# Places given out block by block and token numbers scattered to lists, with three feed-forward groups for the last image

## The chip, the cores and the metric

The kernel runs on one core of a Trainium2 chip. The metric is the device time of one execution in microseconds (us); a kernel's time is the median of its runs. TensorE is written PE, VectorE DVE, ScalarE ACT, GpSimd POOL and SyncE SP, as in the profile.

## The reference

One metaformer layer on x of shape 4 x 256 x 64 x 64, all in float32:

```python
x = x + conv_ref(_ln_c(x))          # three modulated deformable 3x3 convolutions, each with relu
t = _to_tokens(x)                   # 4 images x 4096 tokens x 256 channels
t = t + ffn_ref(_ln_t(t))           # mixture of experts
x = _from_tokens(t, x)
```

Each deformable layer computes offsets and a mask by an ordinary 3x3 convolution (27 outputs), samples its input bilinearly at 9 moved positions per pixel, and multiplies the 9 x 256 samples by its weights. The feed-forward part has 8 experts of 256 -> 512 -> 256 with exact GELU. A softmax over the logits of a gate picks the two best experts of a token and weighs their outputs. The reference computes all experts for all tokens; the kernel computes only the two that count.

## The kernel before

**The convolutions.** An image has 8 blocks of 512 pixels (4 tiles of 128). The list `stages` in `run` (line 1102) sets the order of (layer, image, first block, last block), 96 blocks in all; I write (2,1) 3 for layer 2, image 1, block 3. A block has 9 taps, and `main_block` (line 503) does for each tap 4 gathers, `samples` (515): an indirect DMA on POOL's queue (line 524) brings for each of 128 pixels one table row of 4 KB, two operations on DVE (530, 535) and one on ACT (538) blend it to a sample. There are 9 buffers for gathered tiles (`GB`) and 8 for samples. `turn` (542) transposes pairs of samples on PE (553) and ACT copies them out (556); `share` (562) multiplies them by the weights (570). `finish` (580) applies the ReLU on ACT, two instructions a block (601). `off_block` (358) computes offsets, indices and coefficients for a later block, `store_table` (326) and `enter` (344) write the rows of the next layer's table, `pre_block` (450) loads an image, normalises its pixels over the channels (`normalise`, 58), writes the first table and transposes back (483).

**What is done beside them.** Such work is written as generators. `aside` (1064) puts each one's steps into one of two lists, `side` and `plans_side`; after each tap `step` (1068) takes from each list as many steps as will empty it by the end of the block. So a list of 12 steps gives two in some taps, and a list of `tokens` and `pre_block` steps shares its taps. `after(self.last)` places an instruction behind the newest sampling operation of its engine, `after(self.gathered)` behind the newest gather on POOL.

**Tokens.** After a block of layer 2, `tokens` (611) adds x, transposes to 512 tokens, normalises them, writes them to DRAM (`z`), and computes logits, probabilities, ranks of the experts (`rk`) and the two weights (`cw`).

**The feed-forward part.** The tokens are handled in groups: images 0 to 2 are a group each, image 3 is two groups of 4 blocks. When a group's last block has its ranks, `enqueue` (1026) puts into the lane `routes`: `route` (714), which gives each token its two slots in lists ordered by expert; then for each tile `invert` (827), which turns the slots into the lists of token numbers: two comparisons on DVE (836, 838) make one-hot matrices in float16, and PE multiplies them (842), accumulating in PSUM; then `begin` (1034). A list is cut into units of 128 rows. A group of M tiles has 2M + 7 units, done in steps of two units (a pair) or one (a single): 40 steps and 71 units for an image, 24 steps and 39 units for half of one. `expert` (887) does a step: `fetch` (851) brings on POOL's queue the expert's weights (line 861, unless the same are there already) and one tile of tokens per unit (874); PE transposes them (904) and multiplies (918, 936) with GELU on ACT (928) between. `products` (945) adds the bias on DVE (955) and writes the rows to DRAM. When the group's steps are done, `end` (1043) fills the lane `sums`: for each tile two indirect DMAs on POOL (981) gather its two results (`gy`), DVE adds them with their weights (996), PE transposes (1014), and the rows are written out.

**The pace.** The lanes get one credit per tap (`pump`, 1059). A group's `pace` is the number of taps that a pair takes: 5, 6, 2, 1.5 and 0 for the five groups. At the end of a layer whose next stage needs it (after (1,3) and after (2,3)) `settle` (1079) empties the side lists, and after the last block `drain` (1088) runs what is left. Instructions of an engine run in the order in which the program has them, POOL's DMAs included.

Of the kernel before, what the change touches and what calls it, by code (L numbers as in the profile page):

```python
# [41 lines left out]
NW = 3  # L42
LEAST = 2.0**-30
# [14 lines left out]
def normalise(nc, pool, src, dst, eps, nm):  # L58
# [16 lines left out]
    for _ in range(3):  # L75
        nc.vector.tensor_tensor(sq, rs, rs, ALU.mult)
        nc.vector.scalar_tensor_tensor(sq, sq, -0.5, ve, ALU.mult, ALU.mult)
        nc.vector.scalar_tensor_tensor(rs, sq, 1.5, rs, ALU.add, ALU.mult)
    yield rs
    for t in range(T):  # L80
        nc.vector.tensor_scalar(
            dst[:, t, :], src[:, t, :], mv[:, t, 0:1], rs[:, t : t + 1], ALU.subtract, ALU.mult
        )


class Group:


    def __init__(self, b, n0, n1):
# [8 lines left out]
        self.zt, self.acc, self.gy, self.sums, self.py = {}, [], [], [], None  # L98
        self.order = [self.starts[s % NW] + s // NW for s in range(self.NF)]
# [7 lines left out]
class Lane:  # L107
# [5 lines left out]
    def put(self, taps, fn):  # L113
        self.pieces.append((taps, fn))
# [11 lines left out]
class Weave:  # L126
# [3 lines left out]
    def __init__(self, ctx, tc, ins, out):  # L130
# [29 lines left out]
        self.side, self.plans_side = [], []  # L160
# [58 lines left out]
    def ffn_constants(self):  # L219
# [9 lines left out]
        for g in self.groups:  # L229
            g.zd = self.dram.tile([g.M * P, C], F32, name=f"z_{g.nm}", tag=f"z_{g.nm}")  # L230
        self.ys = [
# [28 lines left out]
        self.fresh = {}  # L260
        for M in {g.M for g in self.groups}:
            fresh = cst.tile([P, E, M], F32, name=f"fresh_{M}")
            nc.vector.memset(fresh, 1.0)
            nc.vector.memset(fresh[:, :, 0:1], 0.0)
            self.fresh[M] = fresh
# [10 lines left out]
        self.token = {}  # L276
        for M in {g.M for g in self.groups}:
            assert M * P // 2 <= 2048
            token = cst.tile([P, M], F32, name=f"token_{M}")
            nc.vector.tensor_scalar(  # L280
                token, self.row_f[:, :M], float(P), self.part, ALU.mult, ALU.add
            )
            nc.vector.tensor_scalar(token, token, float(M * P // 2), None, ALU.subtract)
            self.token[M] = token


# [163 lines left out]
    def pre_block(self, b, n, wins, spare, spill=0):  # L450
# [19 lines left out]
        rest = normalise(nc, self.small, h, h, EPS_C, nm)  # L470
# [140 lines left out]
    def tokens(self, b, n, r):  # L611
# [4 lines left out]
        if n == grp.n0:  # L616
            grp.cw = self.rt2.tile([P, 2, grp.M], F32, tag="cw", bufs=3, name=f"cw_{grp.nm}")
            grp.rk = self.rt2.tile([P, E, grp.M], F32, tag="rk", name=f"rk_{grp.nm}")
        xc = self.big.tile([P, CC, BLK], F32, tag="a", name=f"xr_{nm}")
# [32 lines left out]
        rest = normalise(nc, self.small, tok, z, EPS_T, nm)  # L652
# [54 lines left out]
        for i in range(2):  # L707
            w = small("lg", (P, TPB, E))
            nc.vector.scalar_tensor_tensor(w, rk, float(i), pr, ALU.is_equal, ALU.mult)
            nc.vector.tensor_reduce(grp.cw[:, i, m0 : m0 + TPB], w, AX.X, ALU.add)  # L710
        if n == grp.n1 - 1:
            self.enqueue(grp)

    def route(self, grp):

        nc, M, NF = self.nc, grp.M, grp.NF
        grp.slots = self.rt2.tile([P, 2, M], I32, tag="slots", bufs=3, name=f"slots_{grp.nm}")
        grp.tok = self.rt2.tile([P, grp.NU], I32, tag="tok", name=f"tok_{grp.nm}")
        grp.wrow = self.rt2.tile([P, NF], I32, tag="wrow", name=f"wrow_{grp.nm}")

        def small(tag, shape, dt=F32):
            return self.rt.tile(list(shape), dt, tag=tag, name=f"{tag}_{grp.nm}")

        both = small("r0", (P, E, M))
        nc.vector.tensor_scalar(both, grp.rk, 1.0, None, ALU.is_le)
        rp = self.ps.tile([P, 2, E, M], F32, tag="tp", name=f"rp_{grp.nm}")
        nc.tensor.matmul(rp[:, 0], lhsT=self.upper, rhs=both, start=True, stop=True)
        nc.tensor.matmul(rp[:, 1], lhsT=self.ones, rhs=both, start=True, stop=True)
        tot = small("r1", (P, E, M))
        nc.vector.tensor_copy(tot, rp[:, 1])  # L730
        slot = small("r2", (P, E, M))
        nc.vector.tensor_tensor_scan(
            slot.rearrange("p e m -> p (e m)"),
            self.fresh[M].rearrange("p e m -> p (e m)"),
            tot.rearrange("p e m -> p (e m)"),
            0.0, ALU.mult, ALU.add,
        )

        ni = small("ni", (P, E), I32)
        nc.vector.tensor_scalar(ni, slot[:, :, M - 1], float(P - 1), None, ALU.add)  # L740
# [8 lines left out]
        for v in range(2):  # L749
# [11 lines left out]
        cut = small("cut", (P, E))  # L761
        nc.vector.tensor_scalar(cut, nt[:, 0], float(FT), None, ALU.mult)
        nc.vector.tensor_tensor(off[:, 1], off[:, 1], cut, ALU.subtract)
        nc.vector.tensor_tensor(off[:, 1], off[:, 1], off[:, 0], ALU.subtract)
        nc.vector.tensor_scalar(end[:, 0], end[:, 0], float(FU), None, ALU.mult)
        nc.vector.tensor_scalar(end[:, 1], end[:, 1], base, None, ALU.add)
        nc.vector.tensor_tensor(slot, slot, tot, ALU.subtract)
        nc.vector.tensor_tensor(slot, slot, rp[:, 0], ALU.add)
        every = [P, E, M]
        over = small("r1", (P, E, M))  # L770
        nc.vector.tensor_tensor(over, slot, cut.unsqueeze(2).to_broadcast(every), ALU.is_ge)
        nc.vector.tensor_tensor(
            over, over, off[:, 1].unsqueeze(2).to_broadcast(every), ALU.mult
# [3 lines left out]
            slot, slot, off[:, 0].unsqueeze(2).to_broadcast(every), ALU.add  # L777
# [9 lines left out]

# [6 lines left out]
        part = small("exv", (P, NF))  # L794
        for v in range(2):
            past = small("r1", (P, NF, E))
            nc.vector.tensor_tensor(
                past,
                first.unsqueeze(2).to_broadcast([P, NF, E]),
                end[:, v].unsqueeze(1).to_broadcast([P, NF, E]),  # L800
                ALU.is_ge,
            )
            nc.vector.tensor_reduce(part if v else ex, past, AX.X, ALU.add)
        nc.vector.scalar_tensor_tensor(ex, ex, float(E), ex, ALU.is_lt, ALU.mult)
        nc.vector.tensor_tensor(ex, ex, part, ALU.add)
# [9 lines left out]
        nc.vector.tensor_copy(grp.wrow, rows)  # L815


        grp.digits = []
        for v, (op, k) in enumerate(((ALU.bitwise_and, P - 1), (ALU.logical_shift_right, 7))):
            di = small("di", (P, 2, M), I32)  # L820
            nc.vector.tensor_scalar(di, grp.slots, k, None, op)
            df = small(f"df{v}", (P, 2, M))
            nc.vector.tensor_copy(df, di)
            grp.digits.append(df)
        grp.inv = self.ps1.tile([P, grp.NU], F32, tag="py", name=f"inv_{grp.nm}")

    def invert(self, grp, m):


        nc = self.nc  # L830
        lo, hi = grp.digits
        n = grp.NU
        for i in range(2):
            nm = f"{grp.nm}_{m}_{i}"
            at = self.ffn.tile([P, P], F16, tag="at", name=f"at_{nm}")
            nc.vector.tensor_scalar(at, self.row_f, lo[:, i, m : m + 1], None, ALU.is_equal)
            num = self.ffn.tile([P, n], F16, tag="num", name=f"num_{nm}")
            nc.vector.tensor_scalar(
                num, self.row_f[:, :n], hi[:, i, m : m + 1], self.token[grp.M][:, m : m + 1],
                ALU.is_equal, ALU.mult,  # L840
            )
            nc.tensor.matmul(
# [369 lines left out]
```

## Time and profile before

| What | Value |
|---|---|
| median of 3 runs | 6431.33 us (6419.34 to 6440.2) |
| the profiled execution | 6426.59 us |
| its span, first to last instruction | 6424.5 us |
| mean granted clock of PE | 0.973 |
| software queue (POOL's DMAs): packets, MB, share of 16 engines | 550,240, 1971.12, 81.2% |
| hardware queue (SP's DMAs): the same | 249,136, 270.82, 12.3% |
| HBM traffic over the span | 367 GB/s |

A row of the costliest groups reads: line, engine, operation, written tile <- read tiles, count | busy us in total, mean ns of one | idle time of the engine just before them, and what ended most of it. The page's row of 40 slices gives the busy share in tenths through the run:

```profile
PE   7999999889899999999889999999987999987987
...
POOL 4666776666777767667777776767777764667644
...
DMA  8999999999899999999899999999999996899854
```

Means of single instructions on the lines named above: fetch of weights (861) 1059 ns x168 of POOL's time, of a tile of tokens (874) 1006 ns x291, of results (981) 1081 ns x256; one of the small operations of `tokens` on DVE (709, 128x32) 201 ns.

In time, the last ReLU ends at 6080 us of the span, the last of the products (line 955) starts at 6372 us, and POOL issues the last group's 32 gathers of results from about 6375 to 6415 us.

### The profile page before, as it was taken

The page shows a single profiled execution, that of the slowest core. Times are in us where ns is not written, and L with a number is a line of the kernel's source. Part 1 is how long each engine was busy: PE and PEld are TensorE (multiplying, and loading weights), DVE is VectorE, ACT ScalarE, POOL GpSimd, SP SyncE. Part 2 cuts the span into 40 slices and gives each one's busy share as a digit, 9 for nine tenths or more (in the row PEclk, how much of TensorE's full clock was granted, in tenths as well). Part 3 has the DMA queues.
Part 4 walks back from the last instruction along what each step waited for, and adds up shares of the span by engine and source line. Part 5 has one row for each costly group of instructions (what it writes and reads, how often), then busy time and mean ns, then how long its engine had stood idle before and what let it go on. Part 6 is the DMA issues. An engine that isn't in the chain of part 4 may idle for free.

```text
span 6424.5 us, 88218 instructions
## 1 busy us (share of the span) xinstructions
PE 5903.1 (92%) x26358; PEld 3413.5 (53%) x26358; DVE 4954.5 (77%) x11575; ACT 3298.7 (51%) x7154; POOL 4396.0 (68%) x4215
## 2 busy tenths in 40 slices
PE   7999999889899999999889999999987999987987
PEld 3444444444455555665445555555643566644675
DVE  7988888888977768888877877778988764678621
ACT  3555555555555555555455555555654544454422
POOL 4666776666777767667777776767777764667644
PEclk8999999899999999999999999999999999999998
DMA  8999999999899999999899999999999996899854
GB/s 286 388 370 378 408 404 401 377 361 365 325 393 372 366 340 399 391 355 364 315 356 366 393 380 352 385 368 380 387 369 345 346 338 235 322 335 341 314 179 145
DMA packets 799851, 2247.56 MB, mean 350 GB/s; under 512 B 102184, under 2 KB 300456, under 8 KB 790544
## 3 DMA queue, kind: packets, MB, share of 16 engines
q0 software_dynamic: 550240, 1971.12, 81.2%
q1 hardware_dynamic: 249136, 270.82, 12.3%
q8 instruction: 212, 3.47, 0.2%
q14 instruction: 263, 2.15, 0.1%
HBM read 2166.72 MB, written 191.81 MB: 367 GB/s over the span
## 4 chain that ended last, share of the span: by engine, by line
PE 67%; DVE 11%; DMA 10%; issue 5%; ACT 4%; POOL 2%; SPq 0%; DVEq 0%; ACTq 0%; POOLq 0%
PE acc L570 33%; PE tp L553 9%; DMA g<-tab,idx 8%; PE ph L918 7%; PE py L936 7%; PE po L378 6%; DVE g L530 4%; DVE s L535 3%; ACT s L538 2%; PE pm L392 1%; POOL g L524 1%; PE lp_tok L642 1%; ACT win L601 1%; PE ftp L904 1%; PE tpv L338 1%
## 5 line engine op out<-in xcount | busy, mean ns | idle before, releaser
L524 POOL DMA_INDIRECT g<-tab,idx x3456 | 3625.0, 1049 | 1553.5 <-issue 595.8
L570 PE MATMUL acc<-sT,wk 128*128 128x512 f32 x6912 | 3319.7, 602 | 3.7 <-ACT r L601 1.9
L530 DVE SCALAR_TENSOR_TENSOR g<-g,cf 128x512 f32<-128x512 f32 x3456 | 2561.0, 744 | 348.6 <-DMA g<-tab,idx 341.1
L535 DVE SCALAR_TENSOR_TENSOR s<-g,cf 128x256 f32<-128x256 f32 x3456 | 1656.9, 482 | 480.5 <-PE tp L553 181.0
L538 ACT ACTIVATE s<-s,cf 128x256 f32<-128x256 f32 x3456 | 1664.0, 509 | 642.2 <-DVE s L535 593.8
L570 PEld LDWEIGHTS acc<-sT,wk 128*128 128x128 f32 x6912 | 1195.8, 194 | 818.0 <-issue 801.3
L556 ACT COPY sT<-tp 128x512 f32<-128x512 f32 x1728 | 1011.3, 586 | 1180.0 <-PE tp L553 1167.1
L553 PEld LDWEIGHTS tp<-ident,s 128*128 128x128 f32 x6912 | 867.8, 143 | 1220.0 <-ACT s L538 684.8
L553 PE MATMUL tp<-ident,s 128*128 128x128 f32 x6912 | 1225.1, 282 | 273.0 <-ACT s L538 269.6
L918 PE MATMUL ph<-fzT,w 128*128 128x256 f32 (+1 forms) x2688 | 590.2, 356 | 13.4 <-ACT fzT L908 10.6
L936 PE MATMUL py<-w,hT 128*128 128x256 f32 x2328 | 583.5, 387 | 16.4 <-ACT hT L928 10.4
L918 PEld LDWEIGHTS ph<-fzT,w 128*128 128x128 f32 x2688 | 450.2, 192 | 126.7 <-ACT hT L928 33.5
L928 ACT ACTIVATE hT<-ph,w 128x256 f32<-128x256 f32 (+1 forms) x672 | 266.2, 442 | 467.1 <-PE ph L918 306.2
L936 PEld LDWEIGHTS py<-w,hT 128*128 128x128 f32 x2328 | 425.4, 192 | 136.4 <-issue 47.3
L874 POOL DMA_INDIRECT zt<-z,tok x291 | 292.7, 1006 | 132.4 <-issue 59.2
L981 POOL DMA_INDIRECT gy<-ys,slots x256 | 276.6, 1081 | 105.5 <-issue 65.9
L955 DVE TENSOR_TENSOR y<-py,w 128x512 f32<-128x512 f32 (+1 forms) x168 | 103.3, 615 | 305.2 <-PE py L936 296.7
L861 POOL DMA_INDIRECT w<-in_W,wrow x168 | 177.8, 1059 | 216.9 <-ACT hT L928 45.9
L378 PE MATMUL po<-win,wo 128*32 128x504 f32 (+2 forms) x2560 | 323.8, 551 | 1.5 <-ACT om L387 0.7
L996 DVE SCALAR_TENSOR_TENSOR ta<-gy,cw,ta 128x256 f32<-128x256 f32 x256 | 121.6, 479 | 106.5 <-DMA gy<-ys,slots 87.1
L378 PE MATMUL po<-win_pre,wo 128*32 128x504 f32 (+2 forms) x1280 | 172.0, 572 | 4.0 <-ACT om L387 3.4
L378 PEld LDWEIGHTS po<-win,wo 128*32 128x32 f32 x2560 | 73.1, 109 | 192.0 <-issue 150.1
(171 smaller groups left out, 2836.4 us busy)
## 6 DMA issues: line engine op xcount, KB each, us to landing
tab<-hv SPq DMA_DIRECT2D x512, 128.0 KB
g<-tab,idx POOLq DMA_INDIRECT x3456
tab<-h_pre SPq DMA_DIRECT2D x128, 256.0 KB
ys<-y SPq DMA_DIRECT2D x123, 256.0 KB
wk<-in_conv_w SPq DMA_DIRECT2D x117, 256.0 KB
xc_pre<-in_x SPq DMA_DIRECT2D x32, 512.0 KB
xr_tok<-in_x SPq DMA_DIRECT2D x32, 512.0 KB
t<-t_tok SPq DMA_DIRECT2D x32, 512.0 KB
```

Source lines behind the costliest of these rows:

```text
L378: nc.tensor.matmul(po[g * Q : (g + 1) * Q, :].rearrange("q (r w) -> q r w", w=W)[:, r0:r1, x0:x1], lhsT=self.wo[l][:, 3 * ky + kx, c, :], ...
L524: self.gathered = nc.gpsimd.indirect_dma_start(out=g.rearrange("p x s f -> p (x s f)"), out_offset=None, in_=self.table(*self.stages[i][:2 ...
L530: nc.vector.scalar_tensor_tensor(g[:, :, 0, :], g[:, :, 1, :], cf[:, j, 0:1], g[:, :, 0, :], ALU.mult, ALU.add,)
L535: self.last = nc.vector.scalar_tensor_tensor(s, g[:, 1, 0, :], cf[:, j, 1:2], g[:, 0, 0, :], ALU.mult, ALU.add)
L538: nc.scalar.activation(s, s, AF.Copy, scale=cf[:, j, 2:3])
L553: self.turned = nc.tensor.transpose(tp[:, c, u * P : (u + 1) * P], ss[u][:, c * P : (c + 1) * P], self.ident)
L556: nc.scalar.copy(self.sT[:, :, t0 * P : (t0 + 2) * P], tp)
L570: nc.tensor.matmul(self.acc[:, o, :], lhsT=self.wk[k][:, c, o * P : (o + 1) * P], rhs=sT[:, c, :], start=(k == 0 and c == 0), stop=(k == K ...
L874: self.nc.gpsimd.indirect_dma_start(out=zt, out_offset=None, in_=grp.zd, in_offset=bass.IndirectOffsetOnAxis(ap=grp.tok[:, j : j + 1], axi ...
L918: nc.tensor.matmul(ph[:, h, :n], lhsT=w1[:, o : o + P], rhs=zT[:, c, :n], start=(c == 0), stop=(c == CC - 1),)
L936: nc.tensor.matmul(py[:, u, :], lhsT=hT[h // 2][:, h % 2, u * P : (u + 1) * P], rhs=w2[:, h * C : (h + 1) * C], start=(h == 0), stop=(h == ...
L981: self.nc.gpsimd.indirect_dma_start(out=g, out_offset=None, in_=self.ys[grp.i % 3], in_offset=bass.IndirectOffsetOnAxis(ap=grp.slots[:, i, ...
```

## The change

Places are given out per block: at the end of `tokens` a new generator `place` computes, for the block's 512 tokens, each expert's count and each token's place in a region of 4096 rows per expert, carries the counts on in `full`, and scatters the token numbers to a DRAM array `ids` with eight indirect DMAs of 128 numbers each on POOL's queue. `route` then works only on counts; it finds for each unit the stretch of `ids` that holds its numbers, gathers these with one indirect DMA and transposes them. `invert` is gone. `route` is a generator of six pieces. The last image has three groups, of four, two and two blocks; a group of two blocks has 23 units in 16 steps. The paces are 6, 7.5, 2.4, 1.5, 1.5 and 0. The normalisation in `pre_block` (but for image 0 at the start) is applied by ACT in place of DVE, and `pre_block` and `place` have side lists of their own.

```diff
@@ normalise
+    if scalar:
+        away = pool.tile([P, T], F32, tag="away", name=f"away_{nm}")
+        nc.vector.scalar_tensor_tensor(away, mv[:, :, 0], -1.0, rs, ALU.mult, ALU.mult)
     yield rs
     for t in range(T):
-        nc.vector.tensor_scalar(
-            dst[:, t, :], src[:, t, :], mv[:, t, 0:1], rs[:, t : t + 1], ALU.subtract, ALU.mult
-        )
+        if scalar:
+            nc.scalar.activation(
+                dst[:, t, :], src[:, t, :], AF.Identity,
+                bias=away[:, t : t + 1], scale=rs[:, t : t + 1],
+            )
+        else:
...
@@ pre_block
-        rest = normalise(nc, self.small, h, h, EPS_C, nm)
+        rest = normalise(nc, self.small, h, h, EPS_C, nm, not self.starting)
@@ tokens, at its end
-        if n == grp.n1 - 1:
-            self.enqueue(grp)
+        self.aside(6, self.place(grp, n), place=True)
+
+    def place(self, grp, n):
...
+        both = small("lg", (P, E, TPB))
+        with self.after(self.last):
+            nc.vector.tensor_scalar(both, rk, 1.0, None, ALU.is_le)
+        yield
+        rp = self.ps.tile([P, 2, E, TPB], F32, tag="tp", name=f"rp_{nm}")
+        with self.after(self.turned):
+            nc.tensor.matmul(rp[:, 0], lhsT=self.upper, rhs=both, start=True, stop=True)
+            nc.tensor.matmul(rp[:, 1], lhsT=self.ones, rhs=both, start=True, stop=True)
+        up = small("rp", (P, 2, E, TPB))
+        nc.scalar.copy(up, rp)
+        yield
...
+        put = self.rt2.tile([P, 2, TPB], I32, tag="put", name=f"put_{nm}")
+        nc.vector.tensor_copy(put, sf)
+        ids, key = self.ids[grp.i % 2], f"place_{grp.nm}"
+        for t in range(TPB):
+            if t % 2 == 0:
+                yield
+            for i in range(2):
+                with self.after(self.gathered):
+                    ins = nc.gpsimd.indirect_dma_start(
+                        out=ids,
+                        out_offset=bass.IndirectOffsetOnAxis(ap=put[:, i, t : t + 1], axis=0),
+                        in_=self.token[:, m0 + t : m0 + t + 1],
+                        in_offset=None,
+                    ).ins
+                self.tc.declare_no_dep(ins, group=key, reason="rows of their own")
+                self.tc.add_to_no_dep_group(key, ins)
+                grp.placed.append(ins)
+        if n == grp.n1 - 1:
+            self.enqueue(grp)
@@ route, at its end
-        grp.inv = self.ps1.tile([P, grp.NU], F32, tag="py", name=f"inv_{grp.nm}")
-
-    def invert(self, grp, m):
...
+        lists = small("r0", (P, P))
+        with self.after(self.gathered):
+            ins = nc.gpsimd.indirect_dma_start(
+                out=lists[: grp.NU],
+                out_offset=None,
+                in_=self.ids[grp.i % 2].rearrange("(n a) b -> n (a b)", a=P),
+                in_offset=bass.IndirectOffsetOnAxis(ap=line[: grp.NU, 0:1], axis=0),
+            ).ins
+        for placed in grp.placed:
+            self.tc.add_manual_dep(
+                ins, placed.name,
...
+        tp = self.ps.tile([P, grp.NU], F32, tag="tp", name=f"lists_{grp.nm}")
+        with self.after(self.turned):
+            nc.tensor.transpose(tp, lists[: grp.NU, :], self.ident[: grp.NU, : grp.NU])
+        with self.after(self.last):
+            nc.vector.tensor_scalar(grp.tok, tp, float(M * P - 1), None, ALU.min)
@@ enqueue
         put = self.routes.put
-        put(0, lambda: self.route(grp))
-        for m in range(grp.M):
-            put(0.5 if m else 3, lambda m=m: self.invert(grp, m))
-        put(3, lambda: self.begin(grp))
+        gen = self.route(grp)
+        for taps in range(6):
+            put(min(1, taps), lambda: next(gen, None))
+        put(1, lambda: self.begin(grp))
@@ step
-        for side, taps in ((self.plans_side, K), (self.side, 4 if short else K)):
+        for side, taps in (
+            (self.plans_side, K), (self.side, 4 if short else K), (self.pre_side, K),
+            (self.place_side, K + k),
+        ):
             for _ in range(-(-len(side) // max(1, taps - k))):
                 next(side.pop(0), None)
@@ run
-        self.groups += [Group(last, 0, NB // 2), Group(last, NB // 2, NB)]
+        ends = [0, NB // 2, 3 * NB // 4, NB]
+        self.groups += [Group(last, *part) for part in zip(ends, ends[1:])]
 
-        for i, (g, pace) in enumerate(zip(self.groups, (5.0, 6.0, 2.0, 1.5, 0.0))):
+        for i, (g, pace) in enumerate(zip(self.groups, (6.0, 7.5, 2.4, 1.5, 1.5, 0.0))):
```


## Prediction

> **What bounds the kernel now.** I read the page first: busy shares, the chain, then the costliest groups.
>
> ```profile
> PE 5903.1 (92%) x26358; PEld 3413.5 (53%) x26358; DVE 4954.5 (77%) x11575; ACT 3298.7 (51%) x7154; POOL 4396.0 (68%) x4215
> ...
> PE 67%; DVE 11%; DMA 10%; issue 5%; ACT 4%; POOL 2%; SPq 0%; DVEq 0%; ACTq 0%; POOLq 0%
> ...
> L524 POOL DMA_INDIRECT g<-tab,idx x3456 | 3625.0, 1049 | 1553.5 <-issue 595.8
> ```
>
> TensorE looks like the only bound, and GpSimd looks two thirds busy. The third line warns against that: the gathers are busy 1.05 us each, with 1553.5 us "idle" before them. So I read GpSimd's timeline in a block of stage (2,2), that is layer 2, image 2 (columns: start, duration, engine, line):
>
> ```profile
> 4708.96 0.96 POOL L981 DMA_INDIRECT gy<-ys,slots  x1 [0.30 <-issue]
> 4710.23 1.30 POOL L524 DMA_INDIRECT g<-tab,idx  x1 [0.30 <-DMA g<-tab,idx]
> 4711.84 0.95 POOL L524 DMA_INDIRECT g<-tab,idx  x1 [0.30 <-DVE ta L996]
> 4713.09 0.94 POOL L524 DMA_INDIRECT g<-tab,idx  x1 [0.30 <-DVE pr_tok L692]
> ```
>
> Each gap is the same 0.30 us: GpSimd waits for nobody, it issues back to back, 1.25 us from start to start at best. A DMA costs it that whatever its size (gy moves a quarter of what g moves). From 4700 to 4895 us it issues 139 DMAs, 1.40 us each; from 5104 to 5180 us 57 DMAs, 1.33 us each. I take **1.36 us an issue**, ends 1.30 and 1.40.
>
> Then the busy table by stretch (us, then busy PE, PEld, DVE, ACT, POOL, clock, DMA share, GB/s): a feed-forward stretch, stage (2,0), the stretch around the end of (2,2), the end of the run.
>
> ```profile
> 1985.00:2460.00 475.00, 468.92 (x2067) 276.78 (x2066) 355.43 (x673) 256.63 (x577) 339.32 (x330) 1.00 0.97 364
> ...
> 1186.00:1556.00 370.00, 328.19 (x1397) 182.15 (x1396) 323.72 (x910) 196.81 (x418) 236.30 (x217) 0.91 0.97 363
> ...
> 4669.00:4919.00 250.00, 196.52 (x709) 101.74 (x712) 219.70 (x535) 122.65 (x249) 192.51 (x178) 0.95 0.99 368
> ...
> 6257.00:6354.00 97.00, 93.22 (x470) 76.58 (x469) 11.48 (x22) 29.29 (x75) 38.63 (x40) 1.00 0.53 175
> ```
>
> In the first and last TensorE is full (99%, 96%). In the third it idles 53 us of 250 while GpSimd has 178 issues x 1.36 = 242 us of work: there GpSimd is the bound. So a block of 36 gathers lasts as long as the larger of its TensorE work and 1.36 us times its issues. Block times below are differences between the ends of the second ReLU (line 601) of successive blocks.
>
> **The change, part by part.**
>
> *Inversions go.* By form they are, on VectorE,
>
> ```profile
> L836 DVE TENSOR_SCALAR at<-row_f,df 128x128 f16<-128x128 f32 x256 | 76.0, 297 | 13.0 <-PE inv L842 12.9
> ...
> L838 DVE TENSOR_SCALAR num<-row_f,df,token 128x71 f16<-128x71 f32 x192 | 64.6, 338 | 0.0
> ```
>
> and 20.9 us for the narrow form, 161.5 us in all; on TensorE 40 us. In the body they lie in blocks where TensorE idles 8 to 19 us, so by themselves they pay there nothing. After the last convolution they are bare:
>
> ```profile
> 6126.80:6145.50 18.70, 8.00 (x43) 5.63 (x42) 13.05 (x59) 1.30 (x4) 2.87 (x3) 0.61 0.36 127
> ```
>
> TensorE steps behind VectorE for 18.7 us: **-18.7**.
>
> *Places come.* Per block some 13 small VectorE operations at about 0.2 us (row L709, 201 ns, is such a one): 2.6 us, 83 in all, less than the inversions take; two small matmuls and an ACT copy. And eight scatters on GpSimd's queue: 256 in the run, 256 x 1.36 = 348 us of GpSimd, one to two blocks after each of the 32 layer-2 blocks. No scatter is in the trace. By the rows of the other indirect DMAs (w 1059, zt 1006, gy 1081, g 1049 ns, from 128 KB to 1.2 MB) its issue can't be far from theirs; I give it 1.36 too.
>
> *The wait it adds.* A block's first scatter waits for the slots (`put`) from VectorE. In the order of the built program mostly three gathers have been issued then that VectorE has not yet consumed before `put`; today GpSimd is 4 to 5 ahead in the blocks it bounds, 7 to 8 elsewhere. Behind the waiting scatter stand the next gathers, and VectorE, ACT and TensorE wait for those. A gather's data reach VectorE 7.8 us after issue in (2,2) block 7. The gather three back was issued 4.1 us earlier, so VectorE starts it 3.7 us later, needs 1.2 us for it (744 + 482 ns) and about 1 us for the small ones; GpSimd's own last issue hides 1.36: a wait of 4.6 us, so at most 5. At least 0, if the gathers land sooner once scatters thin the queue. I take the middle, **2.5 us a block**, keeping both ends.
>
> *What the scatters move.* 256 x 128 = 32,768 writes of 4 bytes. The page's software queue gives 81.2% x 16 x 6424.5 us / 550,240 packets = 152 ns a packet, the hardware queue, with packets of 1 KB, 12.3% likewise / 249,136 = 51 ns. So between 0 and 9.7 us a block on each of the 16 engines, 3.2 by the nearer row. In the 8 x 1.36 = 10.9 us that GpSimd spends on scatters it feeds no gather, so they fit: I take 0. The Trainium skill, "DMA: Bandwidth & Descriptors", section Specifications, speaks against this part: under 512 bytes a transfer becomes a read-modify-write. It gives no duration; were the price doubled to the upper end, the sum would be that of the third rival below. No row here shows such a write.
>
> *Paces and the earlier start.* FFN work is spread thinner (pace 5 to 6, 6 to 7.5, 2 to 2.4). A unit (128 rows) costs TensorE 4.2 us: steps whose products stand at 6250 and 6354 us enclose 25 units. Moved units only change where they lie.
>
> *Normalisation of image rows on ACT, with a side list of its own.* In (2,0) TensorE waits for it:
>
> ```profile
> PE tp_pre L483 <- DVE h_pre L81: 44.4, 7, 8.0
> ```
>
> That goes; 96 normalisations of 414 ns leave VectorE for ACT, which has half its time free. But next is GpSimd: 44 issues x 1.36 + 2.5 = 62.3 us against 61.5 a block now.
>
> **The sum,** by issues counted in both program orders (before, after), with 2.5 for each block with a waiting scatter:
>
> - (2,0) block 1: -3. Blocks 2-7: 62.3 x 6 = 374 against 370: +4.
> - (0,1) 2-3: 44 and 45 issues, 126 against 131: -5.
> - (0,1) 4 to (2,1) 1, 16 blocks bound by TensorE: 54 units become 49, -21; idle behind inversions, -7: -28.
> - (2,1) 2-7: 247 issues become 294: 400 + 15 = 415 against 389: +26.
> - (0,2) 2-7: block 2 by TensorE 77, block 3 63.7, the others 193 issues, 262.5: 403 against 416: -13.
> - (0,3) 0 to (1,2) 2: 168 become 189, as gy moves here: 257 against 232: +25.
> - (1,2) 3 to (2,2) 1, 14 blocks: 41 units become 33, -34; GpSimd (39 to 41 issues, 53 to 56 us) lets about two thirds through: -22.
> - (2,2) 2-7: 251 become 288: 392 + 15 = 407 against 344: +63.
> - (1,3) 0-2: 135 issues + 5 = 189 against 198: -9.
> - (1,3) 3 to (2,3) 1: 68 units become 59, -38, but 55 to 58 issues in four of the blocks (75 to 79 us): -27.
> - (2,3) 2-7: 297 become 358: 487 + 15 = 502 against 429: +73.
> - After the last ReLU (6080 us): inversions -18.7; the last group gathers 16 results in place of 32, 16 x 1.26 = -20; 60.5 units in place of 59, +6; fetches queued behind block 7's scatters, 8 x 1.36, +11: -22.
>
> Together **+62**: 6426.6 us (the profiled execution; span 6424.5, 4.7 below the median 6431.3) becomes **6489**. With 1.30 and no wait the same list gives about -138; with 1.40 and 5 us, +247.
>
> **Rivals.**
> 1. *The cover holds* (faster). An issue at 1.30, no wait: then (2,0) falls to TensorE's 57 us a block (-27), (0,2) gives -31, (2,2) costs only +30 and (2,3) +36; with the end the sum lies between -138 and 0, say **6370**. The switch is the wait: near 0, GpSimd's queue stays ahead. For it: GpSimd's true least interval is 1.25 us, and its lead of 7 to 8 gathers in (2,0). Against: 139 issues at 1.40.
> 2. *Losses and gains cancel*: 1.33 and 1.5 us, within 20 us of now, **6430**.
> 3. *Small writes choke the DMA queues*, whose share is already 0.97 to 0.99. At 9.7 us a block, half exposed, 155 more: **6645**, or at 51 ns some 6540 to 6600. Against: GpSimd feeds them slowly.
> 4. *It doesn't do what it says*: the group of blocks 4 and 5 was to be done beside the convolution. In the program's order all 16 of its steps stand behind the last convolution matmul; that is in the sum already.
>
> **How the numbers follow.** Forecast (6445 to 6560) 0.46, cancel 0.13, cover holds 0.29, choke 0.12. Faster by over 0.3% (about what a measurement can tell from no change) 0.29, within 0.13, slower 0.58. The range leaves out the far halves of rivals 1 and 3: 6360 to 6600; the forecast's own is 6445 to 6560.
>
> **What would show it.** Right: blocks (2,2) 2-7 near 68 us and TensorE idle there; (2,3) 4-7 longer; GpSimd waiting 2 to 5 us before each first scatter; scatter issues of about 1 us; the end after the last ReLU near 322 us. Wrong: blocks with 8 scatters no longer than now, or gathers' data much later than 8 us (choke).

## The result and the profile after

The changed kernel takes **7389.62 us** (median of 4 runs, 7387.37 to 7393.88) where the kernel before takes 6429.82 in the same comparison: ratio 1.15, 95% interval 1.1486 to 1.1513. Slower, as forecast, but by 960 us and not by 62: 6489 was predicted, with 6360 to 6600 as the range. In two of the five sets of runs below everything took longer, the kernel before itself 7460 and 7567 us, and no run shows why, so a run is compared only with the kernel before of its own set.

The profiled execution took 7391.46 us, its span is 7389.8. First its page: busy shares, three rows of tenths over the run and the GB/s, then three groups (busy us, mean ns of one | idle before them, and what ended most of it).

```profile
PE 6096.8 (83%) x26414; PEld 3499.6 (47%) x26414; DVE 4943.5 (67%) x11453; ACT 3369.6 (46%) x7334; POOL 4579.3 (62%) x4494
...
PE   7999996567899997677888999976677999766677
...
POOL 5667765455667765455677767754556776455554
...
DMA  9999999998999999899899999998898988889875
GB/s 306 388 360 396 407 403 282 222 255 253 342 368 389 370 392 274 227 264 276 295 360 367 396 367 374 383 299 214 250 269 290 339 317 320 181 239 251 200 177 197
...
L537 POOL DMA_INDIRECT g<-tab,idx x3456 | 3532.8, 1022 | 1819.1 <-issue 629.8
L543 DVE SCALAR_TENSOR_TENSOR g<-g,cf 128x512 f32<-128x512 f32 x3456 | 2570.1, 744 | 1391.8 <-DMA g<-tab,idx 1383.5
...
L779 POOL DMA_INDIRECT ids<-token,put x256 | 265.5, 1037 | 457.2 <-DVE put L772 200.4
```

DVE's wait for gathered rows in the kernel before:

```profile
DVE g L530 <- DMA g<-tab,idx: 341.1, 406, 10.8
```

On POOL and DVE no instruction became dearer: a scatter takes 1037 ns to issue, as guessed, a gather 1022 (1049 before), its blend on DVE 744, as before. What grew is idle time. The PE row has four dips that the row of before does not have, each under a stage of layer 2. And look at the DMA and GB/s rows: in the dips the DMA engines stay at 8 to 9 tenths busy while what they move falls from mostly 340 to 400 GB/s to between 180 and 300. They are occupied, not working. DVE's wait for gathered rows went from 341.1 us to 1383.5.

By stretch, a feed-forward stretch without scatters and the beginning of stage (2,0) (us, busy PE, PEld, DVE, ACT, POOL, clock, DMA share, GB/s):

```profile
1985.00:2460.00 475.00, 469.99 (x2092) 270.48 (x2091) 375.32 (x716) 261.13 (x581) 348.29 (x342) 1.00 0.99 379
1186.00:1556.00 370.00, 220.35 (x888) 116.25 (x887) 205.30 (x577) 126.97 (x274) 170.97 (x166) 0.78 0.90 217
```

In the first nothing changed (before: PE 468.92 of 475). In the second PE works 220 us of 370 where it worked 328, and every other engine works less too: no engine there is the bound. POOL's timeline in the first block with scatters shows what the engines wait for (start, duration, engine, line, idle before and what ended it):

```profile
1188.70 1.27 POOL L779 DMA_INDIRECT ids<-token,put  x1 [7.72 <-DVE put L772]
1190.28 0.98 POOL L779 DMA_INDIRECT ids<-token,put  x1 [0.31 <-issue]
...
1198.30 1.01 POOL L779 DMA_INDIRECT ids<-token,put  x1 [0.30 <-issue]
1199.62 0.99 POOL L779 DMA_INDIRECT ids<-token,put  x1 [0.30 <-issue]
1205.00 0.97 POOL L779 DMA_INDIRECT ids<-token,put  x1 [4.39 <-DMA ids<-token,put]
1211.64 0.97 POOL L779 DMA_INDIRECT ids<-token,put  x1 [5.67 <-DMA ids<-token,put]
1218.83 0.97 POOL L537 DMA_INDIRECT g<-tab,idx  x1 [6.22 <-DMA ids<-token,put]
...
1235.94 0.94 POOL L537 DMA_INDIRECT g<-tab,idx  x1 [12.05 <-DMA ids<-token,put]
1237.18 0.94 POOL L537 DMA_INDIRECT g<-tab,idx  x1 [0.30 <-issue]
1242.56 0.94 POOL L537 DMA_INDIRECT g<-tab,idx  x1 [4.44 <-DMA ids<-token,put]
```

Two waits. The first scatter waits 7.72 us for the slots (`put`), which the prediction had as 2.5, at most 5. The others are new: POOL waits for *scatters to land*. In the built program each of POOL's DMAs waits for the one eight issues before it, so a DMA that lands late stops the queue. The scatter issued at 1190.28 releases the issue of 1205.00, the one of 1191.57 that of 1211.64, the one of 1198.30 that of 1235.94: 512 bytes take 14, 20 and 37 us to land. Over the run (us in total, times, longest):

```profile
POOL g L537 <- DMA ids<-token,put: 327.3, 69, 12.6
...
POOL ids L779 <- DVE put L772: 200.4, 29, 13.9
...
POOL ids L779 <- DMA ids<-token,put: 174.6, 52, 10.5
```

The trace's packet records say what occupied the DMA engines. The scatters' own packets (32 bytes, eight numbers each) are recorded with 15 ns in the median and 17 in the mean. The time stands in the packets of other DMAs: of the 4096-byte packets of POOL's queue, nearly all of them gathers, 1074 took over 1 us before and none over 3, now 4807 and 1023, the longest 17 us. Those over 1 us add up to 802 us per DMA engine (the mean of the 16), before to 86.

### The profile page after: what moved, and what is told of

Its sections match the earlier page's. It is cut to its first block, busy times and chain, and to the rows that moved or that the text cites. A ratio compares the mean times of both kernels' runs of the same rounds, so it can differ in the third digit from the quotient of the medians.

```text
span 7389.8 us, 88842 instructions
## 1 busy us (share of the span) xinstructions
PE 6096.8 (83%) x26414; PEld 3499.6 (47%) x26414; DVE 4943.5 (67%) x11453; ACT 3369.6 (46%) x7334; POOL 4579.3 (62%) x4494
## 5 line engine op out<-in xcount | busy, mean ns | idle before, releaser
L537 POOL DMA_INDIRECT g<-tab,idx x3456 | 3532.8, 1022 | 1819.1 <-issue 629.8
L543 DVE SCALAR_TENSOR_TENSOR g<-g,cf 128x512 f32<-128x512 f32 x3456 | 2570.1, 744 | 1391.8 <-DMA g<-tab,idx 1383.5
L583 PE MATMUL acc<-sT,wk 128*128 128x512 f32 x6912 | 3409.5, 617 | 8.5 <-ACT r L614 6.0
L566 PE MATMUL tp<-ident,s 128*128 128x128 f32 x6912 | 1261.4, 287 | 803.2 <-ACT s L551 790.5
L566 PEld LDWEIGHTS tp<-ident,s 128*128 128x128 f32 x6912 | 893.0, 147 | 1809.5 <-ACT s L551 1225.7
L583 PEld LDWEIGHTS acc<-sT,wk 128*128 128x128 f32 x6912 | 1234.4, 199 | 899.5 <-issue 876.7
L1005 PE MATMUL ph<-fzT,w 128*128 128x256 f32 (+1 forms) x2816 | 634.3, 362 | 44.3 <-ACT fzT L995 19.6
L1023 PE MATMUL py<-w,hT 128*128 128x256 f32 x2384 | 617.7, 391 | 56.2 <-ACT hT L1015 23.7
L1005 PEld LDWEIGHTS ph<-fzT,w 128*128 128x128 f32 x2816 | 478.3, 197 | 159.7 <-issue 38.0
L779 POOL DMA_INDIRECT ids<-token,put x256 | 265.5, 1037 | 457.2 <-DVE put L772 200.4
L991 PE MATMUL ftp<-ident,zt 128*128 128x128 f32 x596 | 101.7, 283 | 96.6 <-DMA zt<-z,tok 96.1
```

The lines of the kernel that those rows point to most:

```text
L537: self.gathered = nc.gpsimd.indirect_dma_start(out=g.rearrange("p x s f -> p (x s f)"), out_offset=None, in_=self.table(*self.stages[i][:2 ...
L543: nc.vector.scalar_tensor_tensor(g[:, :, 0, :], g[:, :, 1, :], cf[:, j, 0:1], g[:, :, 0, :], ALU.mult, ALU.add,)
L566: self.turned = nc.tensor.transpose(tp[:, c, u * P : (u + 1) * P], ss[u][:, c * P : (c + 1) * P], self.ident)
L583: nc.tensor.matmul(self.acc[:, o, :], lhsT=self.wk[k][:, c, o * P : (o + 1) * P], rhs=sT[:, c, :], start=(k == 0 and c == 0), stop=(k == K ...
L1005: nc.tensor.matmul(ph[:, h, :n], lhsT=w1[:, o : o + P], rhs=zT[:, c, :n], start=(c == 0), stop=(c == CC - 1),)
L1023: nc.tensor.matmul(py[:, u, :], lhsT=hT[h // 2][:, h % 2, u * P : (u + 1) * P], rhs=w2[:, h * C : (h + 1) * C], start=(h == 0), stop=(h == ...
```

## Theories and experiments

**Theory 1, neighbours:** the 4-byte writes of numbers that lie beside each other in DRAM get in each other's way and hold up the packets behind them. **Theory 2, issue and wait:** eight issues more and the wait for `put` on POOL's in-order queue. **Theory 3, size:** a write that small is dear wherever it goes. Besides, the rest of the change (normalisation on ACT, side lists, three groups, paces) may gain or lose.

The runs come in five sets, each with the kernel before in it. Where a time is given without an interval, it is one run, and differences under some 20 us (0.3%) say nothing. The edits are shown cut to the lines that matter. Where the lists come from fixed numbers, the kernel does the same amount of work on other tokens, and its output is not the reference's.

### First set (before: 7460 us): size

`e1_no_scatter` leaves out the scatters, and `ids` is filled once with fixed numbers. The other three keep that and scatter to an array of their own, which nobody reads:

```diff
-ids = self.ids[grp.i % 2]
+ids = self.wide[grp.i % 2]                  # e2: E * REG * 128 numbers; e3: rows of 128; e4: rows of 16
-nc.vector.tensor_copy(put, sf)
+nc.vector.tensor_scalar(put, sf, 128.0, None, ALU.mult)         # e2 only
-in_=self.token[:, m0 + t : m0 + t + 1],
+in_=self.row_f[:, :128],                                        # e3; e4: [:, :16]
```

> Leaves out the 256 scatters; the lists are then read from fixed numbers (multiples of 16), so that other tokens are processed. All else of the change stays. If the scatters carry the whole loss, what is left is the sum of the prediction without its 8 issues and its wait per block: about 6245 us, and the blocks (2,2) 2-7 fall from about 93 us to 57 us. If something else of the change carries part of it (the ACT normalisation, the side lists, the paces, the three groups), the time stays above 6490 us.

> The same 256 scatters of 4-byte numbers, but each number goes to a 512-byte row of its own in an array that nobody reads (the lists come from fixed numbers as in the first). Theory size (a write of 4 bytes is slow wherever it goes): as slow as the change, about 7390 us. Theory neighbours (writes of several queues that meet in the same few bytes of DRAM block each other): fast, about 6490 us, the time that the prediction gave for scatters that cost only their issue and a wait of 2.5 us. Theory issue (GpSimd's queue and the wait for put): about 7390 us.

> The same 256 scatters, but each writes 512 bytes of a constant row into a row of its own (the lists come from fixed numbers). Theory size: fast, about 6490 us. Theory neighbours: fast as well, about 6490 us. Theory issue: about 7390 us, since GpSimd issues and waits for the same.

> The same 256 scatters, each writing 64 bytes, rows dense (64 bytes apart; lists from fixed numbers). Theory size with a threshold at 512 bytes: still slow, about 7390 us. Theory size with a price per write that only 4 bytes pay, and theory neighbours with a line of at most 64 bytes: fast, about 6490 us. Between 6600 and 7200 us: neighbours with lines of several 64-byte rows.

Measured: without scatters 7374.96 (0.989 of before there); 4 bytes 512 bytes apart 7952.25 (1.066); rows of 512 bytes 7971.98 (1.069); rows of 64 bytes 7955.74 (1.066). So 4, 64 and 512 bytes cost the same within 0.3%: theory 3 falls here, and in the next set 4-byte writes (e7) again stall nothing. None of the three has 4096-byte packets of over 3 us. The expectations in us suppose a kernel before of 6430 and can't be held against these; the changed kernel itself was not in this set, so it remained open how much of its loss neighbours make.

### Second set (before: 6427.88 us): neighbours, and the rest of the change

`e5_dense_4B` is e2 with a step of 4 bytes in place of 512, all else equal. `e6_no_scatter` and `e7_spread_4B` are e1 and e2 again. `e8_inversions_kept` is the kernel before with everything of the change but the places.

> The changed kernel with its scatters where they were (4 bytes each, neighbouring numbers beside each other), but the lists are read from fixed numbers, as in the no-scatter and the spread kernels (so the output is not the reference's). Theory 1, neighbours: dense 4-byte writes hold up the packets behind them; this one loses about as much as the changed kernel, 1.14 to 1.16 of the kernel before, some 350 to 550 us above the spread kernel of this call, with single packets of over 5 us. Theory 2, issue and wait: the same as the spread kernel within 1%. Theory 3, size of a write: the same as the spread kernel within 1%.

> The changed kernel without its 256 scatters, lists from fixed numbers (so the output is not the reference's), again, beside the others on one chip. If all the loss is in the scatters: 0.96 to 0.99 of the kernel before on this chip. If the rest of the change costs too: over 1.00.

> The scatters write 4 bytes each, 512 bytes apart, lists from fixed numbers (so the output is not the reference's), beside the dense ones. Theory 1: 350 to 550 us below the dense kernel, no packet over 5 us; what it loses to the no-scatter kernel is issue and wait, 32 blocks x 18 us = 580 us, as in the first call. Theories 2 and 3: equal to the dense kernel within 1%.

> The kernel before (inversions, lists from slots) with the rest of the change: normalisation on ACT, the side list of its own, three groups for the last image, the new paces. If the rest is a gain, as blocks without scatters suggest (16 blocks 33 us shorter, 14 blocks 31 us shorter, the end about 20 us shorter): 6340 to 6390 us where the kernel before takes 6430, 0.986 to 0.994 of it. Rival: without the places given out early the thinner pace gains nothing, as the inversions fill the same blocks: within 0.3% of the kernel before.

Measured: dense **7377.43**, spread **6713.04**, none **6362.85**; e8 6406.59, ratio 0.9962 (interval 0.9948 to 0.9977).

The only difference of e5 and e7 is where the 4 bytes go, and it is worth **664 us**, more than the 350 to 550 that were expected: theory 1 is shown. In e7 no 4096-byte packet takes over 3 us (longest 2.5; 1029 take over 3 in e5), and all waits for a scatter to land add up to 1.5 us. The first blocks of (2,0) in e7, in the columns of above:

```profile
1186.00:1556.00 370.00, 300.00 (x1212) 154.93 (x1211) 288.99 (x812) 177.17 (x383) 242.54 (x223) 0.90 0.80 301
```

With the numbers spread, the DMA engines are less busy (0.80 against 0.90) and move more (301 GB/s against 217). The spread scatters still cost 350 us over none, and that is what theory 2 has to explain. Without scatters the rest of the change gains 65 us. Lists read from real scatters add 12 us (7389.62 against 7377.43), within what single runs can't tell. With the inversions kept the rest gains a third of the 65, just above what can be measured and between the two forecasts for e8.

Why `put` costs more than thought is seen in e7, where no dense write disturbs. The wait over the run, and POOL in stage (2,0):

```profile
POOL wide L784 <- DVE put L777: 198.4, 29, 13.9
...
1251.11 1.25 POOL L542 DMA_INDIRECT g<-tab,idx  x1 [0.30 <-DVE lg L746]
1260.10 1.26 POOL L784 DMA_INDIRECT wide<-token,put  x1 [7.74 <-DVE put L777]
```

and DVE in the same microseconds:

```profile
1252.06 0.74 DVE L548 SCALAR_TENSOR_TENSOR g<-g,cf 128x512 f32<-128x512 f32 x1
1252.93 0.48 DVE L553 SCALAR_TENSOR_TENSOR s<-g,cf 128x256 f32<-128x256 f32 x1
1253.34 0.75 DVE L548 SCALAR_TENSOR_TENSOR g<-g,cf 128x512 f32<-128x512 f32 x1
...
1258.17 0.74 DVE L548 SCALAR_TENSOR_TENSOR g<-g,cf 128x512 f32<-128x512 f32 x1
...
1259.65 0.17 DVE L777 TENSOR_SCALAR put<-sf 128x8 int32<-128x8 f32 x1
1259.73 0.74 DVE L548 SCALAR_TENSOR_TENSOR g<-g,cf 128x512 f32<-128x512 f32 x1
```

DVE waits for nothing: it blends one gather after another, 1.28 us from start to start, and no wait for a gather's data shows. Counted in the trace, POOL has issued seven gathers that DVE has not begun when its own last issue ends, and two when the scatter goes out. It is seven and two in 14 of the 32 blocks. `put` stands behind the other five and some of the small operations of `place` (1.3 us here): 5 x 1.28 + 1.3 = 7.7. The wait is DVE's backlog, and it is long because POOL is far ahead. I had worked it out from the arrival of the third gather back.

### Third set (before: 6425.07 us): wait, distance, and a better kernel

`e10_no_put_wait` is e7 with addresses from a constant; `e11_region_per_scatter` and `e12_apart_64B` are e5 with other addresses; `e9_two_groups` is e8 with the two groups of before.

```diff
-ap=put[:, i, t : t + 1]
+ap=self.known[:, 8 * n + 2 * t + i : 8 * n + 2 * t + i + 1]     # e10
-nc.vector.tensor_copy(put, sf)
+nc.vector.tensor_tensor(put, sf, self.apart, ALU.add)           # e11: + E * REG * (4 * i + t)
+nc.vector.tensor_scalar(put, sf, 16.0, None, ALU.mult)          # e12
-(6.0, 7.5, 2.4, 1.5, 1.5, 0.0)
+(6.0, 7.5, 2.0, 1.5, 0.0)                                       # e9, with two groups for the last image
```

> The kernel before with the normalisation on ACT, the side list of its own and the paces 6, 7.5, 2, 1.5, 0; two groups for the last image and the inversions as before. In the kernel with the inversions kept, stages up to (2,2) took 69 us less than before, and the last image's stages and the end 53 us more. If the third group and its pace cost the 53 us: 6350 to 6395 us where before takes 6428, 0.988 to 0.995 of it. If the loss in the last image comes from the work pushed there by the thinner first paces: within 0.3% of the kernel with the inversions kept, 0.996 of before.

> The spread kernel (4 bytes each, 512 bytes apart, fixed lists) with the same eight scatters, but to addresses that stand in a constant from the start, so that no scatter waits for VectorE; the places are still computed (the output is not the reference's). If the wait for the slots costs what it lasts (29 waits of 6.8 us in the spread kernel): 6713 - 198 = 6515 us, to 6550. If the issues alone cost it, as 256 x 1.36 = 348 suggests, and the wait lies beside other work: 6690 to 6715.

> 4-byte writes, fixed lists (so the output is not the reference's); each of the eight scatters of a block writes to a region of its own, so numbers of one scatter still lie beside each other and those of scatters that follow one another never do. If neighbours within one scatter are what stalls: near the dense kernel, 7200 to 7400, packets of over 5 us. If it needs scatters that meet in the same bytes: near the spread kernel, 6700 to 6760, no packet over 5 us.

> 4-byte writes, fixed lists (so the output is not the reference's), 64 bytes apart in place of 512. If only neighbours within 64 bytes stall each other: 6700 to 6730, like the spread kernel. If those within 512 bytes do: over 6900, packets of over 5 us.

Measured: e10 **6562.33**, so the wait costs 151 us of the 350. The other 200 are what is left when nothing waits and nothing stalls, the 256 issues above all; e10 writes to other addresses than e7, which was not tried apart. (In e10 the row of waits for `put` is gone; 198.4 us of waiting in e7 were worth three quarters of their length.) e11 **6792.85**, above the 6700 to 6760 expected: when only numbers of one scatter of a block lie beside each other, 80 of the 664 us are left, and the longest packet takes 5.7 us. So it is chiefly the numbers of different scatters of a block that meet. e12 6715.54: 64 bytes apart is as good as 512. e9 **6374.02**, ratio 0.9921 (interval 0.9908 to 0.9935): by 0.8% it beats the kernel before, and the third group with its paces cost e8 33 us.

### Fourth and fifth set: how near is too near, and the real change mended

`e13_lists_32B` is the whole change, its lists from its scatters, with the numbers 32 bytes apart (an array eight times as large, of whose gathered rows every eighth number is transposed). `e15_lists_32B_later` also puts two taps between `put` and the first scatter. `e14_apart_16B` is e12 with 16 bytes. In the fourth set the kernel before took 7567 us; the fifth has e14 and e15 again (as e17 and e18) beside the changed kernel.

```diff
-nc.vector.tensor_copy(put, sf)
+nc.vector.tensor_scalar(put, sf, 8.0, None, ALU.mult)
+yield                                       # e15 and e18 only
+yield
...
-tp, lists[: grp.NU, :], ...
+tp, lists.rearrange("p (a k) -> p a k", k=8)[: grp.NU, :, 0], ...
```

> The whole change as it is, with the numbers 32 bytes apart in ids (eight times the array, the lists gathered as rows of 4 KB of which every eighth number is used), so the lists come from the scatters again. If 32 bytes are room enough and fixed lists hid nothing: 6700 to 6750 us, no packet over 5 us, 640 us below the changed kernel. If writes 32 bytes apart still meet: over 6850 and long packets. If the lists' dependence on the scatters has its own price: 6750 to 6850 without long packets.

> 4-byte writes 16 bytes apart, fixed lists (so the output is not the reference's). If the stall grows with the number of writes that share 64 bytes (16 when dense, 4 here): between the spread kernel and the dense one, 6750 to 7000. If only the very same 16 bytes count: 6700 to 6730. If any sharing of 64 bytes stalls in full: 7300 to 7400.

> The whole change with the numbers 32 bytes apart and the first scatter two taps after the slots are computed, so that it should find them ready. If the wait costs what the constant addresses saved (151 us): 6560 to 6610 us, 1.02 to 1.03 of before, and no row of waits for put. If the wait only moves to another place on GpSimd's queue: 6690 to 6750, as without the delay. In neither case below the kernel before: 256 issues stay.

Measured, over 7566.92: e13 8113.79 (1.072), e14 8066.63 (1.066), e15 8042.26 (1.0614, interval 1.0589 to 1.0639). None has a 4096-byte packet of over 3 us, and e13, whose lists come from its scatters, stands near the spread kernels of the first set (1.066 to 1.069). The later scatter saves 72 us here. As no dense writes were run in this set, it can't say what the distances are worth.

> The changed kernel as it is, as the mark for the two beside it. On a chip where the kernel before takes 6430 us: 7390, 1.15 of it. On one where it takes 7460 to 7570: if the stalls of dense writes are there too, 1.13 or more and packets of over 5 us; if the slower chip hides them, about 1.07, like the kernel with the numbers 32 bytes apart, and then the kernels measured there say nothing of the distance.

> 4-byte writes 16 bytes apart, fixed lists (so the output is not the reference's), beside the dense ones of the changed kernel. If 16 bytes are room enough: 6700 to 6740 us where before takes 6430 (1.04 to 1.05), or 1.06 to 1.07 where before takes 7460 to 7570, and no packet over 5 us. If a shared 64 bytes still stalls in part: 6750 to 7000, with longer packets.

> The whole change with the numbers 32 bytes apart and the first scatter two taps after the slots are computed. Where before takes 6430: 6560 to 6610 us, 1.02 to 1.03, if both causes are what they seem (stalls 664, wait 151); 6690 to 6750 if the wait moves elsewhere. Where before takes 7460 to 7570: 1.06 again.

Measured, over 6431.39: the changed kernel 7390.61; 16 bytes apart **6737.37**; the whole change with both cures **6534.3**, ratio 1.0161 (interval 1.0144 to 1.0178). That is 856 us off the changed kernel with the same work, the same 256 scatters and 3 MB more of memory traffic, though still above the kernel before, and 26 us below the 6560 to 6610 that were expected. It even lies 28 us under e10, in which no scatter waits either; no run shows why. The wait did not move elsewhere: the largest sum of POOL's waits for DVE, behind `s`, is 228.1 us (212.2 in e7), and in e18's list of POOL's groups the scatters' idle time is 80.0 us, nearly all of it the 0.30 us between any two issues:

```profile
L784 POOL DMA_INDIRECT ids<-token,put x256 | 273.6, 1069 | 80.0 <-issue 67.7 <-DMA g<-tab,idx 7.9 <-DMA w<-in_W,wrow 2.2
```

and in the same stretch of stage (2,0) as above all engines work again:

```profile
1186.00:1556.00 370.00, 327.66 (x1406) 175.57 (x1404) 334.91 (x947) 202.11 (x440) 277.83 (x261) 0.94 0.96 357
```

The distances together, 4-byte writes with lists from fixed numbers (e18: from the scatters; its time has the later scatter in it). The last two columns count the 4096-byte packets of POOL's queue that took over 3 us, and the time of those over 1 us per DMA engine:

| Writes | us | over 3 us | us per engine |
|---|---|---|---|
| none (e6) | 6362.85 | 0 | 75 |
| 512 bytes apart (e7) | 6713.04 | 0 | 76 |
| 64 bytes apart (e12) | 6715.54 | 0 | 81 |
| 32 bytes apart, later (e18) | 6534.30 | 0 | 87 |
| 16 bytes apart (e17) | 6737.37 | 3 | 127 |
| 4 bytes apart, a region for each scatter (e11) | 6792.85 | 127 | 243 |
| 4 bytes apart (e5) | 7377.43 | 1029 | 775 |

Most of the stall needs writes closer than 16 bytes that belong to different scatters of the same block. What in the memory path makes them wait for each other no run shows, and it stays open.

## Why the prediction was wrong, step by step

| Stretch | before | predicted | after | spread (e7) | 32 bytes, later (e18) |
|---|---|---|---|---|---|
| (2,0) 2-7 | 370 | 374 | 566 | 437 | 376 |
| (0,1) 2-3 | 131 | 126 | 170 | 145 | 141 |
| (0,1) 4 to (2,1) 1 | 959 | 931 | 930 | 930 | 940 |
| (2,1) 2-7 | 389 | 415 | 583 | 455 | 402 |
| (0,2) 2-7 | 416 | 403 | 435 | 407 | 395 |
| (0,3) 0 to (1,2) 2 | 232 | 257 | 256 | 259 | 262 |
| (1,2) 3 to (2,2) 1 | 823 | 801 | 797 | 798 | 794 |
| (2,2) 2-7 | 344 | 407 | 558 | 429 | 384 |
| (1,3) 0-2 | 198 | 189 | 240 | 213 | 200 |
| (1,3) 3 to (2,3) 1 | 602 | 575 | 585 | 581 | 586 |
| (2,3) 2-7 | 429 | 502 | 667 | 510 | 488 |
| after the last ReLU | 344 | 322 | 411 | 356 | 366 |

The sum from before to after, by runs: 6428 - 65 (the rest of the change, e6) + 200 (the scatters without wait or stall, e10) + 151 (the wait for `put`, e7) + 664 (neighbours, e5) + 12 (real lists) = 7390.

- **"So they fit: I take 0"** is the step that failed: the DMA price of the 32,768 small writes. It was bounded by 9.7 us a block, 310 us in the run, from the mean time of *a packet*. The dense writes cost 664 us, 21 us a block. The bound failed because a packet's own time was the wrong thing to bound. The scatters' packets are cheap: the trace has 8 a block for each engine, of eight numbers and 17 ns, where the prediction counted 64 of up to 152 ns. The cost is what they do to the packets behind them. Spread, they stall nothing (no packet over 3 us), so 0 would have been right for another layout. Rival 3 (choke) named the effect and gave it 0.12, but priced it by the same rows and so stopped at 6645.
- The rule of the Trainium skill that was weighed there, "DMA: Bandwidth & Descriptors", section Specifications (under 512 bytes a transfer becomes a read-modify-write), does not tell these runs apart: 4 bytes cost the same 64 as 512 bytes apart (6715.54 and 6713.04), and writes of 4 and of 512 bytes differ by 0.25% (1.066 and 1.069 of before). If the rule holds here, it shows no price by itself in these runs; nearness does. Whether near writes stall each other by such read-modify-writes, no run shows.
- **The wait, 2.5 us, at most 5**: 29 waits of 6.8 us on average (198.4 us in e7), the longest 13.9, worth 151 us where some 30 x 2.5 = 75 was meant. What mattered was how far GpSimd is ahead of VectorE, mostly seven gathers, not the landing time of the third gather back.
- **The rest of the sum**: even with the stall gone the change costs 285 us (e7, 6713.04 less 6427.88) and not 62, which is outside the range too. Without the wait as well it costs 137 (e10, 6562.33 less 6425.07), where the list less its 75 us of waits gives -13. So the wait was some 75 us short and the rest of the list some 150.
- **1.36 us an issue, and a block lasts as long as the larger of TensorE's work and GpSimd's issues**: right where there are no scatters, too low in part beside them. The four stretches without scatters, 41 blocks, came within 10 us each of the forecast (931, 257, 801, 575). In e10, where no scatter waits, the blocks (2,2) 2-7 last 1.37 us an issue (395 us for 288), but (2,0) 2-7 last 1.52 (400 us for 263), some 40 us more than 1.36 gives. With both disturbances cured, e18 reaches the last ReLU at 6162 us of its span, and the forecast list gives 6080 + 62 + 22 = 6164. That is closer than it deserves: the list holds some 75 us of waits that e18 does not have, and e18's issues take 1.40 to 1.47 us in (2,0).
- **The normalisation on ACT**: the row of PE's `tp_pre` behind `h_pre` (44.4 us in 7 waits; 42.9 counted from 1186 to 1760 us) shrank to 9.3 in that stretch of e6, now behind ACT, as meant; without scatters the six blocks take 364 us (e6), with the inversions kept 353 (e8). Rival 1's 57 us a block needs 342.
- **After the last ReLU, -22**: came as +9 without scatters (e6, 353) and +67 after. The results' gathers did save what was said: from the last products to the end 31 us in place of 52. But TensorE's idle time after the last ReLU is 77 us in e6 and 74 before, so the 18.7 us of the inversions were lost again. The sum had left out what a third group costs there: with the inversions kept, the end takes 379 us with three groups and their paces (e8) and 346 with two (e9). The dense scatters add 55 us (411 against 356 in e7); in the changed kernel TensorE works 30 us of 86 from 6996 to 7082 us:

```profile
6996.00:7082.00 86.00, 29.70 (x108) 22.64 (x106) 16.60 (x93) 9.90 (x22) 26.42 (x27) 0.64 0.79 71
```

- **What was to show it**: scatter issues of about 1 us, yes (1037 ns); idle TensorE in the layer-2 stages, yes; waits of 2 to 5 us, no, 6.9; (2,2) near 68 us a block, no, 93; the end near 322, no, 411. The sign "gathers' data much later than 8 us" came: DVE's longest wait for a gather is 27.6 us.

In the better kernel, e9, the stretches say where its 0.8% comes from: 16 us in (2,0) 2-7, 27 in (0,1) 4 to (2,1) 1, 22 in (0,2) 2-7, 20 in (1,2) 3 to (2,2) 1, 15 in (2,2) 2-7, and 40 given back at (0,3) 0 to (1,2) 2 and 12 at (2,3) 2-7; that work spread thinner ends later would explain this, but was not tested. How much of it is the normalisation and how much the paces was not tried apart.

## What to carry to other kernels

Don't price a small transfer by its own packet time: ask where its bytes lie and what is queued behind it, and give numbers that are scattered one by one room (here 32 bytes were enough, and 16 nearly). A DMA that waits for another engine's result should be issued late enough to find it ready; on an in-order queue the wait is as long as that engine's backlog, which is longest just where the issuing engine was furthest ahead. And when a change bundles several edits, run each without the others: here one part lost 1027 us (7390 less 6363) and the rest gained 65.

## What the runs showed that was not expected

- Dense 4-byte writes keep the 16 DMA engines busy (0.90 of the time) while 217 GB/s are moved; the share of busy time then says little of throughput. The GB/s row tells.
- Up to 37 us pass until a 512-byte scatter has landed, and as each of POOL's DMAs waits for the one eight before it, this alone costs POOL 502 us of waiting before gathers and other scatters (327.3 + 174.6).
- The granted clock was lower where there were gaps: 0.78 in (2,0) after, 0.94 in the same stretch of e18. PE's busy time is 6096.8 us after and 5932.7 in e18, with the same 26,414 matmuls, so some 160 us of busy time came without more work.
